# A decoder layer on one core: the end of the layer norms on GpSimd, two loads planned anew, and new due-time tables

## The chip, the cores and the metric

The kernel runs on one core of one Trainium2 chip. The metric is the device time of one execution in microseconds (us). A core has TensorE (PE in the profile, its weight loads PEld), VectorE (DVE), ScalarE (ACT), GpSimd (POOL) and SyncE (SP, which here issues nearly all DMAs). Each works through its own queue in order; they wait for each other by semaphores. TensorE writes PSUM, from which VectorE and ScalarE read.

## The reference

x has 4 sequences of 1024 rows of 256 elements. Three blocks follow each other, each on a layer norm without weights:

```python
x = x + attn(layernorm(x))              # causal, 16 heads of 16, cross + shifted scores mixed by a gate
x = x + xattn(layernorm(x), ctx, mask)  # 16 heads over 77 context rows
x = x + ffn(layernorm(x))               # silu(x wg) * (x wu), then wd; hidden size 768, integer weights
layernorm(x) = (x - mean(x)) / sqrt(var(x) + 1e-5)
```

## The kernel before

**Work and stages.** A chunk is 512 rows of one sequence, held as a tile of 128 partitions x 4 x 256; there are 8 chunks (b, n), b from 0 to 3, n 0 or 1. For each chunk the kernel runs:

- `project` (L780): norm of the rows, transposition, k, q and v projections. `spread_rows` (L756) makes each k or q tile: a projection on TensorE (L766), a high half on ScalarE (L729), a low half on VectorE (L732, L734), and eight DMAs on SP (L738) that spread the halves over the partitions.
- `maxima` (L838): scores for the row maxima (L866, causal mask L874), reduced by VectorE (L879); `shift` (L743) makes of them the tile that is subtracted in the next stage.
- `attend` (L903): scores again, keys on partitions (L949, shift L955, mask L962), exponentials on ScalarE (L968), weighted sums (L992, four heads in 32-column tiles), quotients (L679 to L685), output projection (L717) and the residual add on VectorE (L722). The residual x is loaded a second time (L919) and the output bias added on GpSimd (L922).
- `cross_attention` (L1052): norm, q projection and spread, masked maxima (L1106, L1114, L1120), exponentials (L1160, L1162), sums (L1173), output projection and add.
- `ffn` (L1187): norm, transposition into a high and a low half (L1207, L1209), gate and up (L1229), tanh on ScalarE (L1235), two products on VectorE (L1236, L1237), a high half on ScalarE (L1239), a low half on GpSimd (L1240), down (L1263), add (L1269), store (L1272). A first store of x (L1200) serves a branch that is not taken here.

**A norm** is `row_scales` (L148) and `normal_rows` (L163). VectorE takes statistics (L153, L154) of four slices and adds epsilon (L156); GpSimd raises to the power -0.5 (L158; in cross attention it also multiplies by a row mask, L160); VectorE then scales the four 128x256 slices (L166). `to_rows` (L177) transposes them on TensorE (L182).

**What sets the order.** The stages are Python generators. Each yields `piece`s: a TensorE duration, a list `use` of engine times behind it, a time `at` from which it may begin, and buffers that it takes (three PSUM pairs, two singles, six w4, three x and so on). `weave` (L467) keeps a model clock of every engine and always takes the piece that can begin first, moved by the stream's entry in the table LATES (L1290) for its chunk. So costs in `use`, `at` and the tables decide in which order TensorE's instructions are emitted, and that order is kept by hand. In the opening part, until the first maxima have begun, VectorE's order is kept too; after it the framework's scheduler orders the other engines by readiness. The norm's costs are in the list NORM (L696).

Of the kernel before, what the change touches and what calls it, by code (L numbers as in the profile page):

```python
# [8 lines left out]
F32 = mybir.dt.float32  # L9
# [5 lines left out]
ALU = mybir.AluOpType  # L15
# [4 lines left out]
P = 128  # L20
# [7 lines left out]
def tile_decoder_layer(  # L28
# [25 lines left out]
    nc = tc.nc  # L54

    B, S, D = x.shape
# [6 lines left out]
    NG = H // 4  # L63
    NHP = H // 2
    NT = S // P
    CH = 512
    NQ = S // CH
    QT = CH // P
# [16 lines left out]
    def pair():  # L85
        return pp.tile([P, 2, CH], F32, tag="pair", name="pair")

    def single():
        return ps.tile([P, CH], F32, tag="single", name="single")
# [28 lines left out]
    bo_b = const.tile([P, D], F32, name="bo_b")  # L118
# [15 lines left out]
    xpool = ctx.enter_context(tc.tile_pool(name="xpool", bufs=1))  # L134
    w4 = ctx.enter_context(tc.tile_pool(name="w4", bufs=6))
    small = ctx.enter_context(tc.tile_pool(name="small", bufs=2))
    xs = {}

    def x_rows(b, n):
        xt = wide([P, QT, D], "xr")  # L140
        nc.sync.dma_start(xt, x[b, n * CH : (n + 1) * CH, :].rearrange("(t p) d -> p t d", p=P))
        return xt

    def wide(shape, name, dt=F32):

        return w4.tile(shape, dt, tag="w4", name=name)
# [13 lines left out]
            nc.gpsimd.tensor_tensor(rs, rs, keep, ALU.mult)  # L160
        return mv, rs

    def normal_rows(xt, mv, rs, xn=None):  # L163
        xn = xt if xn is None else xn
        for i in range(QT):
            nc.vector.tensor_scalar(  # L166
                xn[:, i, :], xt[:, i, :], mv[:, i, 0:1], rs[:, i : i + 1],
                ALU.subtract, ALU.mult,
            )
        return xn  # L170

    def layer_norm(xt, keep=None):

        mv, rs = row_scales(xt, keep)
        return normal_rows(xt, mv, rs, wide([P, QT, D], "xn"))
# [11 lines left out]
    def transpose_rows(xn):  # L187
        t = to_rows(xn)
        xnT = wide([P, NC, CH], "xnT")
        nc.scalar.copy(xnT, t)  # L190
        return xnT
# [27 lines left out]
    x00 = x_rows(0, 0)  # L219
# [10 lines left out]
    x01 = x_rows(0, 1)  # L230
# [16 lines left out]
    for name, sgn in (("cm_qk", 1), ("cm_kq", -1)):  # L247
        t = masks_f[name] = stage.tile([P, P], BF16, name=name + "f")
# [55 lines left out]
    first = row_scales(x00)  # L304
    bvx = stage.tile([P, NC, P], F32, name="bvx")
    nc.vector.tensor_copy(bvx, bvn.unsqueeze(2).to_broadcast([P, NC, P]))
    normal_rows(x00, *first)

    def transposed(src, n, put):

# [16 lines left out]
    t = single()  # L327
# [3 lines left out]
    for ec in range(NC):  # L331
        t = single()
# [8 lines left out]
    t = single()  # L341
# [10 lines left out]
    t = single()  # L352
# [104 lines left out]
    def give(token, when):  # L457
        pool, k = token
        pool.free[k] = when

    def piece(pe, use=(), at=0.0, cond=None, free=(), mode="whole", **take):

        return dict(pe=pe, use=use, at=at, cond=cond, free=free, mode=mode, take=take)
# [227 lines left out]

        return rest

    NORM = [("DVE", 2.6), ("POOL", 1.1), ("DVE", 1.7)]  # L696

    def out_proj(st, nat, t_nat, w, xt):

# [80 lines left out]
    def project(st, b, n):  # L780

        if (b, n) == (0, 0):
            yield piece(0.0, w4=1)
            xnT, t_x, at = x00T, st.got["w4"], 0.0
        else:
            yield piece(
                0.0, use=[("DMA", 4.0)] * (b > 0) + NORM, w4=1,
                cond=lambda: (("half", b - 1) if b else ("projected", 0, 0, 0)) in flags,
            )
            t_xn = st.got["w4"]  # L790
            xn = x01 if (b, n) == (0, 1) else x_rows(b, n)
            normal_rows(xn, *row_scales(xn))
            flags.add(("normal", b, n))
            yield piece(
                1.1, use=[("ACT", 1.05)], at=st.done + LATE, pair=1, w4=1, free=t_xn
            )
            xnT = transpose_rows(xn)
            st.release("pair")
            t_x = st.got["w4"]
            at = st.done + LATE  # L800
        for c in range(NC):
            kT[b, n, c] = yield from spread_rows(
                st, wkT, xnT, c, bkp, (0, 1, 0, 1), 1.0, "k", at
            )
            qT[b, n, c] = yield from spread_rows(
                st, wqT, xnT, c, bqp, (0, 0, 1, 1), 1.0, "q", at, None,
                t_x if c == NC - 1 else (),
            )
            flags.add(("projected", b, n, c))
            if c == 0:  # L810
                for i in range(QT):
                    if i % 2 == 0:
                        yield piece(
                            2.0, use=[("ACT", 1.8)] if i else [],
                            cond=lambda: (b, n) != (0, 0) or ("normal", 0, 1) in flags,
                            **({} if i else {"pair": 1, "v": 1}),
                        )
                        if i == 0:
                            t_pair, t_v = st.got["pair"], st.got["v"][0]
                            vs = qk.tile(  # L820
                                [P, QT, H * V1 + W - V1], F32, tag="v", name="vs", bufs=NQ
                            )
                            nc.gpsimd.memset(vs, 1.0)
                            t = pair().rearrange("p a (i d) -> p (a i) d", d=D)
                    for k in range(NC):
                        nc.tensor.matmul(
                            t[:, i, :], xnT[:, k, i * P : (i + 1) * P], wvT[:, k, :],
                            start=(k == 0), stop=(k == NC - 1),
                        )
                give(t_pair.pop(), st.done)  # L830
                for i in range(QT):
                    nc.scalar.copy(
                        vs[:, i, : H * V1].rearrange("p (h w) -> p h w", w=V1)[:, :, 0:HD],
                        t[:, i, :].rearrange("p (h w) -> p h w", w=HD),
                    )
                vT[b, n] = vs, t_v, st.done + LATE
# [66 lines left out]
    def attend(st, b, n):  # L903
# [6 lines left out]
        for g in range(NG):  # L910
            c = g // 2
            if g % 2 == 0:
                yield piece(0.0, cond=lambda: (b, n, c) in shifts and (b, n) in vT and "selections" in flags)
                ms, at, t_ms = shifts.pop((b, n, c))
                if g == 0:
                    yield piece(0.0, x=1, use=[("DMA", 4.0)])
                    xt = xpool.tile([P, QT, D], F32, tag="x", name="x", bufs=3)
                    xs[b, n] = xt, st.got["x"][0]
                    nc.sync.dma_start(  # L919
                        xt, x[b, n * CH : (n + 1) * CH, :].rearrange("(t p) d -> p t d", p=P)  # L920
                    )
                    nc.gpsimd.tensor_tensor(  # L922
                        xt, xt, bo_b.unsqueeze(1).to_broadcast([P, QT, D]), ALU.add
                    )
                q, t_q, _ = qT.pop((b, n, c))
                over = [t_ms, t_q]
                if n == NQ - 1:
                    over += [kT[b, m, c][1] for m in range(NQ)]
            acc = []
            for kb in range(nk):  # L930
# [7 lines left out]
                for p in range(2):  # L938
                    yield piece(
                        0.04 + w * 8.2e-4 + (0.11 if diag else 0.0), mode="rows", pair=1, es=1,  # L940
                        at=at,
                        use=[("ACT", 0.1 + w * 1.85e-3)],
# [3 lines left out]
                    t = pair()  # L946
# [54 lines left out]
                lag.append(weigh)  # L1001
                if len(lag) > 1:
                    yield from lag.pop(0)()
                if tails and kb == 1:
                    nat, t_nat = yield from quotients(st, tails.pop(), nat, t_nat)
        yield from lag.pop()()
        nat, t_nat = yield from quotients(st, tails.pop(), nat, t_nat)
        yield from out_proj(st, nat, t_nat, woT, xt)
        flags.add(("attended", b, n))

    def quotients(st, tail, nat, t_nat):
        rest, toks, at, g = tail
        yield piece(
            0.55, use=[("DVE", 0.75)], at=at, single=1, free=toks,
            **({"w4": 1} if nat is None else {}),
        )
        if nat is None:
            nat, t_nat = wide([P, QT, D], "nat"), st.got["w4"][0]
        rest(nat, g)
        st.release("single")  # L1020
        return nat, t_nat
# [30 lines left out]
    def cross_attention(st, b, n):  # L1052
        yield piece(
            0.0, use=NORM, w4=1,
            cond=lambda: ("attended", b, n) in flags and "cross weights" in flags,
# [131 lines left out]
    def ffn(st, b, n, xt=None, rest=()):  # L1187
# [6 lines left out]
        yield piece(  # L1194
            0.0, use=NORM, w4=1, cond=lambda: ("crossed", b, n) in flags and all(("ffn weights", m) in flags for m in range(3)),
        )
# [82 lines left out]
    def every(part, lates, chunks=range(NQ)):  # L1279
# [8 lines left out]
        return Stream(pieces, lates)  # L1288

    LATES = (  # L1290
        [0.00, 0.00, 0.00, 0.00, -0.03, 0.00, -0.31, 0.00],
        [0.00, 0.00, 0.00, 0.00, 0.00, 0.00, -0.23, 0.00],
        [0.00, 0.00, 0.00, 0.00, 0.00, 0.00, 0.00, 0.00],
        [-1.02, 0.03, 0.00, -0.48],
        [0.54, 0.47, 0.00, 0.31],
        [-0.20, -0.15, -0.42, -0.02, 0.00, 0.33, 0.00, 0.00],
    )
    streams = [
        every(maxima, LATES[0]), every(cross_attention, LATES[1]), every(attend, LATES[2]),
# [13 lines left out]
    t = single()  # L1313
# [6 lines left out]
    with tc.If(over_v > 0):  # L1320
# [8 lines left out]
        for b in range(B):  # L1329
            for n in range(NQ):  # L1330
                xt = xpool.tile([P, QT, D], F32, tag="x", name="x", bufs=3)
# [35 lines left out]
```

## Time and profile before

| what | us |
|---|---|
| median of three timed runs | 1229.28 (1228.77 to 1231.69) |
| the profiled execution | 1232.86 |
| its span, first to last instruction | 1231.1 |
| TensorE busy | 1110.8 |
| VectorE busy | 729.9 |
| ScalarE busy | 562.6 |
| GpSimd busy | 130.8 |

The mean granted TensorE clock is 0.958. Busy time of TensorE is modelled from pipelined matmuls. In the profile a line of a group reads: line, engine, operation, tile written <- tiles read, shapes, count, busy time, mean ns of one, and the idle time of the engine ahead of them with what ended it. A line of the timeline reads: start, duration, engine, line, operation, tiles, shapes, count, and in brackets the idle time ahead of it and what ended that. In a line of the waits stand the waiting instruction, what it waited for, total us, times, longest.

### The profile page before, as it was taken

What the parts mean: (1) busy time and instruction counts of PE and PEld (TensorE: products, weight loads), DVE (VectorE), ACT (ScalarE), POOL (GpSimd) and SP (SyncE); (2) the same over time, 40 slices, a digit from 0 to 9 for tenths busy, and PEclk for the clock granted to TensorE, in tenths of its full rate; (3) what the DMA queues carried; (4) which work ended last, traced back from release to release, by engine and by line L of the source; (5) the groups of instructions that cost most, each with busy time, mean ns of one, the idle gap of its engine ahead of it and who ended that gap; (6) DMA issues with size and microseconds to landing.
All of it is one profiled execution on the core that took longest, in us unless ns stands there. A gap on an engine that the chain in (4) does not pass through costs nothing. (4 is left out here: it accounts for less than half of the span.)

```text
span 1231.1 us, 22029 instructions
## 1 busy us (share of the span) xinstructions
PE 1110.8 (90%) x9059; PEld 684.9 (56%) x9059; DVE 729.9 (59%) x1247; ACT 562.6 (46%) x801; POOL 130.8 (11%) x138
## 2 busy tenths in 40 slices
PE   6679989999999898999898998999999889996875
PEld 4445544557555466557555456556575545565654
DVE  5566786354687856255777856347458666136342
ACT  3044544654434463753353563653535336661521
POOL 4031000002000012001100002000110000011212
PEclk9798999999999999999999998999999989998986
DMA  6992315537732016555533015444826140006000
GB/s 124 130 201 63 58 33 69 69 53 92 97 55 40 9 38 110 75 71 87 87 52 38 8 42 70 85 63 60 102 44 91 36 63 8 18 1 86 1 35 19
DMA packets 65438, 76.44 MB, mean 62 GB/s; under 512 B 22451, under 2 KB 39399, under 8 KB 65332
## 3 DMA queue, kind: packets, MB, share of 16 engines
q1 hardware_dynamic: 64227, 74.62, 39.1%
q8 instruction: 73, 1.20, 0.5%
q10 hardware_dynamic: 1104, 0.35, 0.1%
q14 instruction: 34, 0.27, 0.1%
HBM read 15.28 MB, written 9.33 MB: 20 GB/s over the span
## 5 line engine op out<-in xcount | busy, mean ns | idle before, releaser
L968 ACT ACTIVATE es<-pair 128x1024 f32<-128x1024 f32 (+3 forms) x384 | 300.8, 812 | 252.6 <-PE pair L962 178.4
L879 DVE TENSOR_REDUCE mt<-pair 128x2 f32<-128x1024 f32 (+3 forms) x384 | 351.4, 952 | 92.3 <-PE pair L874 60.8
L866 PE MATMUL pair<-k,q 64*128 64x512 f32 (+3 forms) x768 | 163.2, 428 | 29.8 <-DVE mt L879 12.6
L949 PE MATMUL pair<-q,k 64*128 64x512 f32 (+3 forms) x768 | 161.4, 417 | 22.4 <-DVE mt L879 16.5
L992 PE MATMUL single<-es,vs 128*32 128x512 f32 (+3 forms) x1536 | 166.2, 506 | 0.1
L866 PEld LDWEIGHTS pair<-k,q 64*128 64x128 f32 x768 | 76.0, 188 | 121.4 <-DVE mt L879 41.7
L955 PE MATMUL pair<-ms,sel 64*128 64x512 f32 (+3 forms) x768 | 134.6, 347 | 0.0
L949 PEld LDWEIGHTS pair<-q,k 64*128 64x128 f32 x768 | 73.2, 187 | 102.6 <-issue 34.8
L1240 POOL TENSOR_TENSOR hT<-h,hT 128x512 fp32r<-128x512 f32 x48 | 61.4, 1280 | 306.8 <-ACT hT L1239 297.2
L1162 ACT ACTIVATE es<-pair 77x1024 f32<-77x1024 f32 x64 | 63.4, 1020 | 45.8 <-PE pair L1160 45.5
L955 PEld LDWEIGHTS pair<-ms,sel 64*128 64x128 f32 x768 | 74.2, 190 | 3.1
L1120 DVE TENSOR_REDUCE mx<-pair 128x8 f32<-128x616 f32 x64 | 48.7, 794 | 43.7 <-PE pair L1114 43.7
L1263 PE MATMUL pair<-wdT,hT 128*128 128x256 f32 x384 | 63.3, 320 | 11.6 <-POOL hT L1240 4.8
L158 POOL TENSOR_TENSOR rs<-ve,mhalf 128x4 f32<-128x4 f32 x24 | 24.3, 1012 | 439.5 <-DVE ve L156 439.4
L1235 ACT ACTIVATE h<-pair 128x512 f32<-128x512 f32 x48 | 28.7, 598 | 89.0 <-PE pair L1229 84.8
L874 PE MATMUL pair<-cm_qk,id 64*128 64x64 bf16 (+1 forms) x1024 | 69.0, 211 | 0.0
L962 PE MATMUL pair<-cm_kq,id 64*128 64x64 bf16 (+1 forms) x1024 | 67.3, 211 | 0.0
L1236 DVE SCALAR_TENSOR_TENSOR h<-h,pair 128x512 f32<-128x512 f32 x48 | 33.0, 687 | 57.5 <-ACT h L1235 57.2
L1263 PEld LDWEIGHTS pair<-wdT,hT 128*128 128x128 f32 x384 | 55.8, 216 | 18.4 <-POOL hT L1240 6.3
L1114 PE MATMUL pair<-k2s,q 128*128 128x156 f32 x256 | 46.7, 308 | 12.1 <-DMA q<-hi 5.3
L992 PEld LDWEIGHTS single<-es,vs 128*32 128x32 f32 x1536 | 32.4, 109 | 40.7 <-issue 29.6
L674 ACT COPY aS<-single 128x512 f32<-128x512 f32 x64 | 37.5, 589 | 31.6 <-PE single L992 19.0
(180 smaller groups left out, 1575.0 us busy)
## 6 DMA issues: line engine op xcount, KB each, us to landing
q<-hi SPq DMA_DIRECT2D x128, 128.0 KB, 5.1
q<-lo SPq DMA_DIRECT2D x128, 128.0 KB, 6.3
k<-hi SPq DMA_DIRECT2D x64, 128.0 KB, 4.3
k<-lo SPq DMA_DIRECT2D x64, 128.0 KB, 6.0
xr<-in_x_dram SPq DMA_DIRECT2D x8, 512.0 KB, 6.0
x<-in_x_dram SPq DMA_DIRECT2D x8, 512.0 KB, 7.4
x_dram<-x SPq DMA_DIRECT2D x8, 512.0 KB, 2.6
out_dram<-x SPq DMA_DIRECT2D x8, 512.0 KB, 3.7
```

What stands on the lines that cost most here:

```text
L866: nc.tensor.matmul(t[:, j, :w], q[r, a, i * P : (i + 1) * P], k[r, a, :w], start=True, stop=True,)
L874: nc.tensor.matmul(t[:, j, w - P + 64 * half : w], id2[r, half], cm_qk[r, half, 64 * half :], start=False, stop=True, skip_group_check=True,)
L879: nc.vector.tensor_reduce(mt[:, i, :, p, kc], t[:, :, :w], AX.X, ALU.max)
L949: nc.tensor.matmul(t[:, j, lo:], k[r, a, ki * P : (ki + 1) * P], q[r, a, lo:], start=True, stop=False,)
L955: nc.tensor.matmul(t[:, j, lo:], sel[r, hp, :], ms[r, lo:], start=False, stop=True)
L962: nc.tensor.matmul(t[:, j, lo : lo + 64 * (half + 1)], id2[r, half], cm_kq[r, half, : 64 * (half + 1)], start=False, stop=True, skip_group ...
L968: nc.scalar.activation(es[:, :, lo:], t[:, :, lo:], AF.Exp)
L992: nc.tensor.matmul(acc[0][W * jj : W * (jj + 1), lo:], vs[:, ki, V1 * h : V1 * h + W], both[jj // 2][:, jj % 2, lo:], start=(kb == 0), sto ...
L1120: nc.vector.tensor_reduce(mt[:, i, h4 : h4 + 4, :].rearrange("q (k p) j -> q k (p j)", k=2), tv[:, :, :, :S2], AX.X, ALU.max,)
L1162: nc.scalar.activation(es[:S2], t[:S2], AF.Exp)
L1240: nc.gpsimd.tensor_tensor(hs[:, 1, :], h, hs[:, 0, :].bitcast(F32), ALU.subtract)
L1263: nc.tensor.matmul(t[:, i, :], h[1][:, v, i * P : (i + 1) * P], w[:, h[0], :], start=(m == 0), stop=(m == len(terms) - 1),)
```

## The change

The scalings that end a norm move from VectorE to GpSimd, in the same queue as the root; only the very first chunk's norm keeps VectorE. The list NORM books this. In `project` the load of x is one piece, booked at 6.5 us where it was 4.0, and the norm's work a second piece that may begin when the load is done. In `attend` the piece that takes an x buffer and loads the residual stands after the first key block of the last head group and no longer at the stage's start, and the bias add is a piece of its own ahead of the last quotients. The entries of LATES are others.

```diff
-    def normal_rows(xt, mv, rs, xn=None):
+    def normal_rows(xt, mv, rs, xn=None, eng=nc.gpsimd):
         xn = xt if xn is None else xn
         for i in range(QT):
-            nc.vector.tensor_scalar(
+            eng.tensor_scalar(
                 xn[:, i, :], xt[:, i, :], mv[:, i, 0:1], rs[:, i : i + 1],
                 ALU.subtract, ALU.mult,
             )
...
-    normal_rows(x00, *first)
+    normal_rows(x00, *first, eng=nc.vector)
...
-    NORM = [("DVE", 2.6), ("POOL", 1.1), ("DVE", 1.7)]
+    NORM = [("DVE", 2.4), ("POOL", 3.4)]
...
             yield piece(
-                0.0, use=[("DMA", 4.0)] * (b > 0) + NORM, w4=1,
+                0.0, use=[("DMA", 6.5)] * (b > 0), w4=1,
                 cond=lambda: (("half", b - 1) if b else ("projected", 0, 0, 0)) in flags,
             )
             t_xn = st.got["w4"]
-            xn = x01 if (b, n) == (0, 1) else x_rows(b, n)
+            xn = x_rows(b, n) if b else x01
+            yield piece(0.0, use=NORM, at=st.done)
             normal_rows(xn, *row_scales(xn))
...
-                if g == 0:
-                    yield piece(0.0, x=1, use=[("DMA", 4.0)])
-                    xt = xpool.tile([P, QT, D], F32, tag="x", name="x", bufs=3)
-                    xs[b, n] = xt, st.got["x"][0]
-                    nc.sync.dma_start(
-                        xt, x[b, n * CH : (n + 1) * CH, :].rearrange("(t p) d -> p t d", p=P)
-                    )
-                    nc.gpsimd.tensor_tensor(
-                        xt, xt, bo_b.unsqueeze(1).to_broadcast([P, QT, D]), ALU.add
-                    )
...
                 if len(lag) > 1:
                     yield from lag.pop(0)()
+                if g == NG - 1 and kb == 0:
+                    yield piece(0.0, x=1, use=[("DMA", 6.5)])
+                    xt = xpool.tile([P, QT, D], F32, tag="x", name="x", bufs=3)
+                    xs[b, n] = xt, st.got["x"][0]
+                    nc.sync.dma_start(
+                        xt, x[b, n * CH : (n + 1) * CH, :].rearrange("(t p) d -> p t d", p=P)
+                    )
+                    x_at = st.done
...
         yield from lag.pop()()
+        yield piece(0.0, use=[("POOL", 1.5)], at=x_at)
+        nc.gpsimd.tensor_tensor(xt, xt, bo_b.unsqueeze(1).to_broadcast([P, QT, D]), ALU.add)
         nat, t_nat = yield from quotients(st, tails.pop(), nat, t_nat)
...
     LATES = (
-        [0.00, 0.00, 0.00, 0.00, -0.03, 0.00, -0.31, 0.00],
-        [0.00, 0.00, 0.00, 0.00, 0.00, 0.00, -0.23, 0.00],
-        [0.00, 0.00, 0.00, 0.00, 0.00, 0.00, 0.00, 0.00],
-        [-1.02, 0.03, 0.00, -0.48],
-        [0.54, 0.47, 0.00, 0.31],
-        [-0.20, -0.15, -0.42, -0.02, 0.00, 0.33, 0.00, 0.00],
+        [0.00, 0.00, 0.00, 0.00, -0.51, 0.00, 0.00, 0.00],
+        [0.00, -0.23, 0.00, 0.00, 0.00, 0.00, -0.05, -0.74],
+        [0.02, 0.00, 0.00, 0.00, 0.00, 0.00, 0.00, 0.04],
+        [0.43, -0.16, 0.00, -0.24],
+        [0.59, 0.33, 0.00, 0.14],
+        [0.00, 0.00, -0.63, -0.14, 0.00, 0.42, -0.76, 0.08],
     )
```

## The prediction

> **What bounds the kernel now.** I read the engine table first, then stretches, then who waited for whom, then the timeline at the largest holes.
>
> ```profile
> PE 1110.8 (90%) x9059; PEld 684.9 (56%) x9059; DVE 729.9 (59%) x1247; ACT 562.6 (46%) x801; POOL 130.8 (11%) x138
> ```
>
> ```profile
> 0.00:100.00 100.00, 72.08 (x531) 45.24 (x532) 59.51 (x125) 28.77 (x52) 25.51 (x46) 0.85 0.83 140
> 100.00:1100.00 1000.00, 943.22 (x8040) 567.53 (x8041) 609.47 (x1013) 498.10 (x696) 80.35 (x71) 0.98 0.38 58
> 1100.00:1231.00 131.00, 95.46 (x490) 72.13 (x489) 60.94 (x110) 35.73 (x53) 24.91 (x21) 0.85 0.18 33
> ```
>
> The second fence is busy time by stretch (columns PE, PEld, DVE, ACT, POOL, clock, DMA share, GB/s). TensorE sets the end: in the middle 1000 us it idles 56.8 us at a granted clock of 0.98; start and end hold another 28 and 36 us, at 0.85. VectorE is 59% busy, GpSimd 11%. So VectorE work taken away is worth only what TensorE waits for it.
>
> ```profile
> PE pair L949 <- DVE mt L879: 16.5, 22, 3.8
> PE pair L866 <- DVE mt L879: 12.6, 16, 3.2
> ...
> L166 DVE TENSOR_SCALAR xn<-x,mv,rs x64: 395/407/2407, 152.2 to 1187.4; 128x256 f32<-128x256 f32 x64
> ```
>
> Waits for the row maxima L879 are the largest group (us, times, longest): they free the PSUM pairs that TensorE writes next. The L166 row is the four scalings that end a norm: median 0.407 us, longest 2.407. The holes:
>
> ```profile
> 984.47 2.34 POOL L922 TENSOR_TENSOR x<-x,bo_b 128x1024 f32<-128x1024 f32 x1
> 984.55 3.38 DVE L166 TENSOR_SCALAR xn<-x,mv,rs 128x256 f32<-128x256 f32 x4 [0.95 <-POOL rs L160]
> 988.59 0.79 PE L949 MATMUL pair<-q,k 64*128 64x512 f32 x2 [3.80 <-DVE mt L879]
> ...
> 480.25 0.64 PE L1114 MATMUL pair<-k2s,q 128*128 128x156 f32 x4 [2.60 <-DMA q<-lo]
> 763.01 1.11 PE L1114 MATMUL pair<-k2s,q 128*128 128x156 f32 x4 [2.94 <-issue]
> ...
> 1187.03 1.94 PE L182 MATMUL pair<-ident,xn 128*128 128x128 f32 x8 [4.93 <-DVE xn L166]
> ```
>
> At 984 VectorE waits 0.95 us for GpSimd's root, then one scaling lasts as long as the GpSimd add beside it (2.41 against 0.41 us), the maxima queue behind, and TensorE stands for 3.80 us. A like hole of 1.85 us ends at 198.31. The two L1114 holes are something else: the q that cross attention spreads by DMA has not landed. At 1187 the last norm lies bare on the path.
>
> **Off VectorE (gain).** 23 of 24 norms lose 4 x 0.407 = 1.63 us of VectorE each, 37 us in all, its waits for the root (22 us) and the twelve stretched scalings (12 us over their median, each beside a GpSimd instruction). Nearly all of that has cover: around most norms TensorE does not idle at all. I count the two holes that end in it, **-5.7 us**; bounds 0 (the maxima are late again) and -23 us (every middle hole that ends at L879).
>
> **Onto GpSimd (cost).** No row shows such a scaling on GpSimd. One-input rows of L641 (1.04, 0.83, 0.62 us for 1024, 768, 512 elements) give 0.41 us for 256; the two-input rows L922 and L1240 (2.37 and 1.28 us) give 0.74. I take 0.55, nearer the one-input rows since only one operand is a tile: 2.2 us for four, between 1.6 and 2.9. A norm's path from the last L717 matmul becomes add 1.22 + statistics 2.4 + root 1.0 to 1.2 + 2.2 = 7.0 us, 0.6 longer than with VectorE. The new TensorE order, laid out with the trace's spacings (0.23 us a feed-forward matmul, 0.43 an L717 one), puts 11 us or more between that matmul and the transposes, 8.6 at the last cross attention: covered. Bare is only the last norm: **+0.4** (transposes follow the scalings one by one; -0.2 to +1.0).
>
> The Trainium skill (GPSIMD Engine Reference, "Engine selection") speaks against the move: elementwise work belongs on VectorE, GpSimd being about twice as slow with two inputs and near line rate with one. By twice the VectorE row the four would last 3.3 us, an estimate that adds 1.1 us at the last norm alone: the sum would be a microsecond smaller.
>
> What queues behind: GpSimd also makes the low halves L1240 (48 x 1.28 us), for which TensorE waits 4.8 us now. With 50 us more on a 131 us queue, these waits grow: **+2** (0 to +12, if each of 24 pairs met half a microsecond).
>
> **Another order on TensorE.** The tables and the new pieces re-plan everything; the two orders hold the same matmuls line by line (1792 of maxima, 2560 of scores, 1152 + 1152 of feed-forward). Two things can be counted.
>
> First, changes of array layout (64-row tiles, 32-column tiles, whole array) fall from 681 to 634. The trace prices them as start-to-start time beyond the median spacing: leaving columns 0.35 us, rows to columns 0.08, rows to whole 0.12, whole to rows 0.03. With 4, 8, 14 and 25 fewer (and 4 more from whole to columns at 0.03): 1.4 + 0.6 + 1.7 + 0.8 - 0.1 = **-4.4 us**; bounds 0 (waits lie in these means) and -6.
>
> Second, the distance from a q projection to its first use. In the two L1114 holes the projection ended at 468.3 and 751.0 and the data landed 12.0 us later, with only 8.5 us of TensorE work ordered between. In the new order the shortest such distance in the middle is 11.6: **-5.5 us** (-6 to 0, if other q tiles come late in turn). At the last cross attention the two distances go from 6.7 and 5.9 to 7.6 and 7.8 us against holes of 5.33 and 1.26 us: **-1.0** (-2 to 0).
>
> Against it, the PSUM pairs are taken more densely: stretches in which four are claimed within about 2 us of TensorE work rise from 251 to 286 (middle). Now TensorE waits 34 us in the middle for L879, L968 and L1162 to free a pair, 0.135 us per such stretch: 35 x 0.135 = **+4.7** (0 to +9).
>
> **The start.** The second chunk's v projection (3.40 and 1.99 us before 62 us, at a low clock) and its last k projection (1.98 at 62.8) move behind the first exponentials: 6.0 us at full clock. Walking VectorE's rows forward (eight maxima, 3.5 us of selections, q's low half, seven maxima, a 1.2 us maximum of weights, k's) the first exponential comes at 63 instead of 65.3. Left are 4 us, half of which fit the 6.9 us that TensorE idles from 65 to 100: **+2** (-2 to +6).
>
> **x read late, costs of transfers.** Nothing by themselves: the load of x is still issued when one of three buffers comes free, in the same neighbourhood of SP's queue (behind the output store of an earlier chunk), and the add stays on GpSimd. Its 155.9 us of waiting there (longest 43.8) held no norm up: VectorE never waited more than 1.5 us for a root. The booked 6.5 us fit the measured landings (6.0 and 7.4).
>
> **Sum**: -5.7 + 0.4 + 2 - 4.4 - 5.5 - 1.0 + 4.7 + 2 = -7.5 us. The profiled execution took 1232.86 (span 1231.1 and 1.8 around it), 3.6 above the median 1229.28; it would become 1225.4, the median 1221.8.
>
> **Rivals.**
> *The holes go and nothing fills them*: without the 4.7 and the two costs of 2 the sum is -16.2, with 2 more from L879 -18: 1229.3 - 18 = 1211. For it: VectorE gets 60 us freer just where maxima queue. Against: TensorE is at 94% there.
> *The waits only move*: the denser pair use and new late q tiles take back what the old holes gave, 1229. For it: such a plan is made from booked durations, and 144 small holes now sit all over the middle.
> *GpSimd's queue becomes the wait* (slower): it works in order, and in the new order five of the eight adds of x stand directly ahead of a norm. A norm has about 4 us of slack (11 less 7.0); an add whose transfer is still under way takes up to 7.4 + 2.37, so 5.8 us of TensorE each. Three such: 1221.8 + 17.4 = 1239; from two on it decides. Against: the same five neighbourhoods exist now without harm.
>
> **Chances.** Forecast 0.46 (own range 1216 to 1226), nothing fills the holes 0.16, waits only move 0.16, GpSimd's queue 0.22. About 0.3%, 3.7 us, is what a measurement of this kernel can tell from no change. Faster 0.44 + 0.16 = 0.60; same 0.16 + 0.02 = 0.18; slower 0.22. The range 1209 to 1240 leaves out the outer ends of the first and last rival, under 2 in 10.
>
> **What will show it.** L166 on GpSimd at 0.41 to 0.74 us; no stretched scaling on VectorE; VectorE near 681 us busy, GpSimd near 181; middle idle of TensorE from 57 to some 52 us (the layout changes pass as busy time), with no 2.6 us hole ahead of L1114; first exponential before 65 us; the last bare norm hole 4.7 to 5.9 us. Wrong, if transposes L182 wait for GpSimd, if L1263 waits for L1240 by more than 10 us, or if the middle idles over 60 us.

## The result and the profile after

The changed kernel takes 1261.67 us (median of four, 1260.21 to 1268.34) where the kernel before takes 1229.03 beside it: 1.0271 times as long (95% interval 1.0232 to 1.0310), 32.6 us slower. The forecast was 1221.8, range 1209 to 1240. Its profiled execution took 1261.28 us, with a span of 1259.5 against 1231.1.

Line numbers of the changed kernel are one higher than before's from L788 on, nine lower in the scores of `attend` (scores L940, exponentials L959, weighted sums L983), and one higher again behind them (bias add L1007, products L1237 and L1238, low half of h L1241, down L1264).

The engine table's first line, and the busy time by stretch (columns PE, PEld, DVE, ACT, POOL, clock, DMA share, GB/s):

```profile
PE 1110.7 (88%) x9059; PEld 682.5 (54%) x9059; DVE 690.0 (55%) x1155; ACT 561.7 (45%) x801; POOL 241.9 (19%) x230
```

```profile
0.00:100.00 100.00, 68.93 (x544) 42.62 (x545) 58.29 (x126) 28.86 (x51) 30.26 (x50) 0.88 0.73 130
100.00:1100.00 1000.00, 922.79 (x7829) 553.75 (x7828) 570.81 (x922) 483.68 (x679) 171.04 (x146) 0.98 0.39 59
1100.00:1260.00 160.00, 119.00 (x689) 86.12 (x689) 60.92 (x108) 49.12 (x72) 40.65 (x34) 0.88 0.16 31
```

TensorE does the same work in the same busy time at the same clock: 1110.7 us for 9059 matmuls. VectorE got 40 us freer, as meant. But in the middle 1000 us TensorE now idles 77.2 us where it idled 56.8. Between its first and its last matmul its holes grew from 105.0 to 132.3 us, and these 27.3 are nearly all of the 28.4 us that the span grew. The time went into waits. Who waited for whom in the changed kernel, then two rows of the kernel before:

```profile
PE pair L867 <- DVE mt L880: 17.0, 29, 2.7
PE pair L940 <- DVE mt L880: 15.8, 26, 2.9
PE pair L182 <- POOL xn L166: 15.0, 15, 5.7
...
PE pair L867 <- DVE h L1238: 6.0, 4, 2.1
```

```profile
PE pair L182 <- DVE xn L166: 6.1, 2, 4.9
...
PE pair L1263 <- POOL hT L1240: 4.8, 6, 1.0
```

The waits for row maxima, which the freer VectorE was to shorten, stand at 32.8 us in these two rows instead of 29.1. Transposes wait 15.0 us for GpSimd's scalings where they waited 6.1 for VectorE's. A wait that was small before, for the product h on VectorE, holds the maxima's scores up. Summed over all waiting lines, holes ended by h went from 2.2 to 10.6 us, by cross attention's maxima mx from 1.9 to 6.7, by the packed maxima mpad from 0.6 to 5.9. In the middle 1000 us alone, holes ended by the maxima grew from 23.1 to 31.0 us.

The row of the scalings (least, median, longest ns):

```profile
L166 POOL TENSOR_SCALAR xn<-x,mv,rs x64: 1217/1220/1227, 151.3 to 1216.2; 128x256 f32<-128x256 f32 x64
```

One takes 1.220 us, 3.0 times VectorE's 0.407 and more than twice the 0.55 that I took. Four and the root last about 6 us; the changed NORM books 3.4.

The start, and the last norm, in TensorE's timeline:

```profile
60.61 0.89 PE L747 MATMUL single<-ident,mpad 128*128 128x128 f32 x4 [4.74 <-DVE mpad L888]
...
1213.89 0.69 PE L182 MATMUL pair<-ident,xn 128*128 128x128 f32 x2 [5.75 <-POOL xn L166]
1215.10 0.69 PE L182 MATMUL pair<-ident,xn 128*128 128x128 f32 x2 [0.52 <-POOL xn L166]
```

The first is a new hole. The last norm's hole grew from 4.93 to 5.75 us, and after the first transposes TensorE stands about half a microsecond for each further scaling.

### The profile page after: what moved, and what is told of

Its sections match the earlier page's. It is cut to its first block, busy times and chain, and to the rows that moved or that the text cites. A ratio compares the mean times of both kernels' runs of the same rounds, so it can differ in the third digit from the quotient of the medians.

```text
span 1259.5 us, 22081 instructions
## 1 busy us (share of the span) xinstructions
PE 1110.7 (88%) x9059; PEld 682.5 (54%) x9059; DVE 690.0 (55%) x1155; ACT 561.7 (45%) x801; POOL 241.9 (19%) x230
## 4 chain that ended last, share of the span: by engine, by line
PE 33%; DVE 9%; POOL 4%; issue 3%; ACT 3%; DMA 2%; SPq 0%; POOLq 0%; ACTq 0%; DVEq 0%
PE single L983 5%; DVE mt L880 5%; PE pair L940 4%; PE single L766 3%; PE pair L867 2%; PE pair L1161 2%; PE pair L717 2%; POOL xn L166 2%; PE pair L946 2%; PE pair L1230 2%; PE pair L1264 2%; DMA q<-lo 2%; PE single L679 2%; PE pair L182 1%; PE single L1174 1%
## 5 line engine op out<-in xcount | busy, mean ns | idle before, releaser
L959 ACT ACTIVATE es<-pair 128x1024 f32<-128x1024 f32 (+3 forms) x384 | 300.5, 811 | 253.7 <-PE pair L953 179.9
L940 PE MATMUL pair<-q,k 64*128 64x512 f32 (+3 forms) x768 | 160.8, 416 | 22.9 <-DVE mt L880 15.8
L983 PE MATMUL single<-es,vs 128*32 128x512 f32 (+3 forms) x1536 | 163.5, 497 | 0.5 <-ACT aS L674 0.5
L940 PEld LDWEIGHTS pair<-q,k 64*128 64x128 f32 x768 | 72.4, 185 | 105.8 <-issue 44.3
L1241 POOL TENSOR_TENSOR hT<-h,hT 128x512 fp32r<-128x512 f32 x48 | 61.2, 1275 | 267.8 <-ACT hT L1240 243.0
L166 POOL TENSOR_SCALAR xn<-x,mv,rs 128x256 f32<-128x256 f32 x64 | 77.3, 1221 | 1.7
L1264 PE MATMUL pair<-wdT,hT 128*128 128x256 f32 x384 | 62.2, 316 | 9.1 <-POOL hT L1241 3.8
L1237 DVE SCALAR_TENSOR_TENSOR h<-h,pair 128x512 f32<-128x512 f32 x48 | 32.9, 686 | 66.0 <-ACT h L1236 65.9
L953 PE MATMUL pair<-cm_kq,id 64*128 64x64 bf16 (+1 forms) x1024 | 66.7, 209 | 0.0
L684 DVE RECIPROCAL rd<-single 128x16 f32<-128x16 f32 x64 | 16.2, 254 | 88.5 <-PE single L679 88.4
L1264 PEld LDWEIGHTS pair<-wdT,hT 128*128 128x128 f32 x384 | 54.9, 213 | 15.1 <-POOL hT L1241 5.1
L1007 POOL TENSOR_TENSOR x<-x,bo_b 128x1024 f32<-128x1024 f32 x8 | 18.9, 2366 | 212.7 <-DMA x<-in_x_dram 179.1
```

Of the source, the lines that this page charges most:

```text
L166: eng.tensor_scalar(xn[:, i, :], xt[:, i, :], mv[:, i, 0:1], rs[:, i : i + 1], ALU.subtract, ALU.mult,)
L940: nc.tensor.matmul(t[:, j, lo:], k[r, a, ki * P : (ki + 1) * P], q[r, a, lo:], start=True, stop=False,)
L953: nc.tensor.matmul(t[:, j, lo : lo + 64 * (half + 1)], id2[r, half], cm_kq[r, half, : 64 * (half + 1)], start=False, stop=True, skip_group ...
L959: nc.scalar.activation(es[:, :, lo:], t[:, :, lo:], AF.Exp)
L983: nc.tensor.matmul(acc[0][W * jj : W * (jj + 1), lo:], vs[:, ki, V1 * h : V1 * h + W], both[jj // 2][:, jj % 2, lo:], start=(kb == 0), sto ...
L1241: nc.gpsimd.tensor_tensor(hs[:, 1, :], h, hs[:, 0, :].bitcast(F32), ALU.subtract)
```

## The experiments

Two things changed at once: which engine scales, and the order in which everything is emitted, since `piece`s, bookings and tables all feed the planner. My first theory was **price**: the loss is GpSimd's 1.220 us, booked too low. The rival was **order**: the re-planned order is slower whoever scales. Times are medians; ratios are to the kernel before on the same chip, with 95% intervals.

### Price or order

**e1_after_vector** keeps the changed kernel's order of TensorE, ScalarE and SyncE, with the scalings on VectorE.

```diff
-    def normal_rows(xt, mv, rs, xn=None, eng=nc.gpsimd):
+    def normal_rows(xt, mv, rs, xn=None, eng=nc.vector):
```

> The changed kernel with its scalings L166 back on VectorE; booked costs, tables and so the order of TensorE, ScalarE and SyncE are those of the changed kernel, instruction by instruction. Theory (price): the four scalings on GpSimd, 4.9 us where the plan books 2.4, make the loss of 32 us; with VectorE (1.63 us) most of it goes: 1225 to 1238. Rival (order): the new order of TensorE is itself worse, whoever scales: 1250 to 1262. In between, both have a part.

Measured: 1261.17 us, 1.0251 (1.0205 to 1.0297). **Price** falls: the same order without any scaling on GpSimd is as slow. Its waits show what the order does alone:

```profile
PE pair L867 <- DVE mt L880: 18.6, 30, 2.7
PE pair L940 <- DVE mt L880: 17.6, 27, 4.1
...
PE pair L867 <- DVE h L1238: 8.0, 4, 3.5
PE pair L1115 <- DMA q<-lo: 6.2, 2, 4.4
```

The wait for xn is back at its old size (6.1 us), but those for maxima (36.2 in two rows against 29.1) are longer than in either kernel. Those for q, both halves over all lines, are 17.0 us against 16.5 in either. So in this order GpSimd's scalings do shorten the waits for maxima, from 39.0 to 35.4 us over all lines, and lengthen those of the transposes, from 7.9 to 18.6; the medians do not differ.

**e2_before_gpsimd** is the reverse: before's order, with the scalings (all but the first chunk's) on GpSimd.

```diff
-    def normal_rows(xt, mv, rs, xn=None):
+    def normal_rows(xt, mv, rs, xn=None, eng=nc.gpsimd):
...
-            nc.vector.tensor_scalar(
+            eng.tensor_scalar(
```

> The kernel before with nothing changed but the engine of the scalings (GpSimd but for the first chunk); the order of TensorE, ScalarE and SyncE is that of the kernel before. Theory (price): each norm gets 3.2 us longer in an order made for the short norm, so about as much is lost as in the changed kernel: 1248 to 1265. Rival (order): GpSimd's price is hidden there, 1229 to 1236.

Measured: 1244.71 us, 1.0117 (1.0069 to 1.0164). That lies between the ranges of the two theories: in before's order GpSimd's price is 15.6 us, half the loss. e2's waits:

```profile
PE pair L182 <- POOL xn L166: 17.9, 17, 5.7
PE pair L1263 <- POOL hT L1240: 13.0, 7, 4.4
PE pair L866 <- DVE mt L879: 12.7, 17, 3.2
PE pair L949 <- DVE mt L879: 11.1, 20, 0.7
```

My gain is there to the tenth: holes ended by the maxima over all lines fell from 31.5 to 25.8 us, 5.7, and the two holes that I had counted are the ones that went. It is outweighed at xn (17.9 against 6.1) and at the low half hT (13.0 against 4.8). GpSimd's timeline of e2 shows how the second comes about:

```profile
469.11 3.63 POOL L166 TENSOR_SCALAR xr<-xr,mv,rs 128x256 f32<-128x256 f32 x3
472.70 1.26 POOL L1240 TENSOR_TENSOR hT<-h,hT 128x512 fp32r<-128x512 f32 x1
473.95 1.22 POOL L166 TENSOR_SCALAR xr<-xr,mv,rs 128x256 f32<-128x256 f32 x1
```

Three scalings hold the queue for 3.63 us, the low half comes after them, and TensorE's down projection stands for 4.37 us where it stood 0.63.

**e4_forms** asks what the 1.220 us consists of. Each of a norm's four scalings has another form, so the rows are not normalised: two operations with per-partition operands (as the change has it), one such operation, two operations with constants, one with a constant.

```diff
+            elif i == 1:
+                eng.tensor_scalar(xn[:, i, :], xt[:, i, :], rs[:, i : i + 1], None, ALU.mult)
+            elif i == 2:
+                eng.tensor_scalar(xn[:, i, :], xt[:, i, :], 0.01, 1.01, ALU.subtract, ALU.mult)
+            else:
+                eng.tensor_scalar(xn[:, i, :], xt[:, i, :], 1.01, None, ALU.mult)
```

> The changed kernel with four forms of scaling in one norm, to price them on GpSimd: slice 0 as it is (two operations, two scalars read from SBUF), slice 1 one multiplication by a scalar read from SBUF, slice 2 two operations with constants, slice 3 one multiplication by a constant. Slices 1 to 3 leave out the true mean and scale, so the output is another. If the 1.22 us lies in the scalars read from SBUF, slice 0 is 1.22, slice 1 about 0.8 and slices 2 and 3 about 0.41, as the one-input rows of the casts say; if each operation costs a pass, slices 0 and 2 are 1.22 and slices 1 and 3 about 0.6 to 0.7; if it is the price of a scaling in any form, all are 1.22.

The four forms on GpSimd (count | busy us, mean ns | idle before):

```profile
L167 POOL TENSOR_SCALAR xn<-x,mv,rs 128x256 f32<-128x256 f32 x16 | 19.7, 1230 | 1.7
...
L174 POOL TENSOR_SCALAR xn<-x 128x256 f32<-128x256 f32 x16 | 17.3, 1083 | 180.0 <-DVE x L729 180.0
L172 POOL TENSOR_SCALAR xn<-x,rs 128x256 f32<-128x256 f32 x16 | 14.9, 930 | 0.0
L176 POOL TENSOR_SCALAR xn<-x 128x256 f32<-128x256 f32 x16 | 13.7, 858 | 0.0
```

None of the three cases that I had set out came. The plainest form, one operation with a constant, already takes 858 ns. A second operation adds 0.23 to 0.30 us, per-partition operands 0.07 to 0.15. The casts from which I took 0.41 us are no neighbours of this instruction.

**e3_booked_6** tells the changed kernel's planner the truth and leaves its tables.

```diff
-    NORM = [("DVE", 2.4), ("POOL", 3.4)]
+    NORM = [("DVE", 2.4), ("POOL", 6.1)]
```

> The changed kernel with 6.1 us booked for GpSimd's part of a norm (root 1.0, mask 0.2, four scalings 4.9) instead of 3.4; tables kept. Theory (price): once the plan knows the price it puts other work ahead of the transposes and gets part of the loss back: 1238 to 1255, and TensorE waits less than 5 us for L166 outside the last norm (15 and 3.5 us in the changed kernel). Rival (order): no better than 1255 to 1270.

Measured: 1336.86 us, 1.0875 (1.0830 to 1.0920). A true booking made it 75 us slower still. No theory had that: the planner answers to a small change of cost with another order altogether.

### One part at a time

That gave a third theory, **fit**: six rows of tables are right for one set of costs and pieces only, and any other pair of them draws an order with more holes. Rivals: **tables** (the new rows are bad) and **late x** (reading x late costs).

**f1_tables_only**: before with the new LATES, nothing else. **f2_after_old_tables**: the changed kernel with the old LATES, scalings on VectorE. Both swap the block of the change's diff. **f3_late_x_only** and **f4_pieces_only** take over, with the old LATES and VectorE, the hunk of `attend`, or the hunks of NORM and `project`.

> The kernel before with the changed kernel's six rows of LATES and nothing else (x early, one norm piece with its old bookings, scalings on VectorE). 'Fit' theory (tables and bookings are good only together, any new pair of them draws another order that idles more): 1240 to 1265 us. 'Tables' rival (the new rows themselves are bad): 1255 to 1270 here, and the run with the old rows in the changed kernel falls back to about 1229. 'Late x' rival (the late read carries the loss): within 5 us of 1229.

> The changed kernel with the old rows of LATES and with its scalings on VectorE (so to be set beside the 1261 us of the changed order with VectorE). 'Fit': still slower than before, 1240 to 1290 us, since the rows no longer fit the pieces. 'Tables': 1229, within 5. 'Late x': 1255 to 1265, as with the new rows.

> The kernel before with x for the sums read late (load issued after the last scores of a chunk, the add of bo in a piece of its own behind the last weighted sums), old rows, old norm piece, VectorE. 'Late x': 1250 to 1262 us, with the wait for L1007's add or for GpSimd on its path. 'Tables': within 5 us of 1229. 'Fit': 1235 to 1260, with the idle time spread over the waits for row maxima and for q's low half and none of it at x.

> The kernel before with the norm's piece split in two (transfer booked 6.5 us, then root and scalings at its landing, booked DVE 2.4 and POOL 3.4), old rows, x early, scalings still on VectorE. 'Fit': 1235 to 1265 us. 'Tables' and 'late x': within 5 us of 1229.

| | us | ratio |
|---|---|---|
| f1, new tables alone | 1292.62 | 1.0517 (1.0474 to 1.0561) |
| f2, all but the tables | 1352.70 | 1.1011 (1.0981 to 1.1041) |
| f3, late x alone | 1331.94 | 1.0838 (1.0809 to 1.0867) |
| f4, norm pieces and bookings alone | 1313.78 | 1.0705 (1.0675 to 1.0734) |

Every part alone loses 65 us or more, and the parts together without the tables 125. So the new tables are no culprit: they bring the new pieces from 1352.7 to 1261. Only fit had all four slow, and all four lie above its ranges too. Part of the size goes with the clock, as f2's stretches show against before's 0.85 and 0.98:

```profile
0.00:100.00 100.00, 63.26 (x420) 40.28 (x420) 51.29 (x116) 23.48 (x43) 23.81 (x45) 0.81 0.83 136
100.00:1200.00 1100.00, 981.19 (x8050) 591.13 (x8048) 611.77 (x1020) 495.87 (x696) 81.72 (x73) 0.95 0.35 53
```

f2's TensorE is busy 1156.7 us for the same 9059 matmuls that took 1110.8, and idle for 195.3 us of its span where before's is for 120.3. Its mean granted clock is 0.923 for 0.958. The five versions that idle most, e3 and f1 to f4 (157.6 to 195.3 us), were granted 0.923 to 0.943 in their profiled executions, all others 0.944 to 0.961. That the idle time brings the clock down is not shown.

### Other tables for the same code

Is the changed code slower by itself, or only as far as its tables go? I ran the kernel's own `weave` with many tables and kept those whose planner clock (the end of its last piece, a number of the planner and not a time of the chip) was near that of the two kernels, 1220.9 for before and 1217.0 for the change. For e3 it stands at 1297.9 and for f1 to f4 at 1322.3, 1320.9, 1323.1 and 1308.8: the planner itself finds these orders long, so they say little of the changed kernel, whose order it finds short and which is slow on the chip all the same. Only rows of LATES differ within a code and its bookings:

```diff
-        [-1.02, 0.03, 0.00, -0.48],
-        [0.54, 0.47, 0.00, 0.31],
+        [0.00, 0.00, 0.02, -0.25],
+        [0.03, 0.04, 0.13, 0.38],
```

(two of the six rows, for g3). g1 and h2 also book the change truly, NORM on GpSimd 6.1 and the add of bo 2.4; g2 puts the scalings on VectorE; g4 has x early.

> Control: the kernel before, nothing changed but LATES, found anew from zeros by the planner's clock until it stood at 1220.0 us there (before's own rows: 1220.9). 'Fit': 1240 to 1265 us, although code and bookings are before's. 'Misbooked' and 'change's own cost': 1222 to 1237.

> A second set of rows found by the planner's clock for the code of before, at 1224.6 us there; the first, at 1220.0, took 1239.9. 'Fit': 1235 to 1270. 'Change's own cost': 1225 to 1245, below both sets of the changed code.

> The changed kernel with its bookings set to what the trace shows (NORM on GpSimd 6.1 instead of 3.4, the x add 2.4 instead of 1.5) and LATES found anew for these bookings by the planner's own clock (1225.5 us there; 1217.0 for the changed kernel, 1220.9 for before). 'Misbooked' theory (the changed plan loses because it holds GpSimd's norms for shorter than they are): the waits of L182 for GpSimd fall from 18.5 to under 10 us and the time returns to 1225 to 1240. 'Fit' theory (a plan that is found on the planner's clock alone comes out 20 to 45 us above that clock on the chip, whatever its norms do): 1240 to 1270. 'Change's own cost' rival (late x, or GpSimd behind the root, costs 30 us in any order): 1255 to 1270, with this run slower than the control with before's code by 20 or more.

> A second set of rows of LATES for the changed kernel with true bookings (6.1 and 2.4), at 1218.8 us on the planner's clock; the first, at 1225.5, took 1248.2. 'Fit': anything from 1235 to 1270, unlike the first by 5 us or more, so that the set of rows and not the norms decides. 'Change's own cost': 1248 to 1262, and both sets above both sets of before's code.

> The changed kernel with its own bookings (NORM on GpSimd 3.4) and other rows of LATES, at 1213.2 us on the planner's clock, 3.8 below the changed kernel's rows. If the planner's clock could rank plans this near each other, 1257; 'Fit': anywhere from 1240 to 1280. 'Misbooked': as slow as the changed kernel or slower, with 15 us or more of waiting for L166 again.

> Late x and the split norm piece as in the changed kernel, but the scalings on VectorE, booked as three steps (DVE 2.4, POOL 1.1, DVE 1.7), and LATES found anew for that (1215.0 us on the planner's clock). 'Misbooked': near 1229, within 8. 'Fit': 1235 to 1265, no matter that nothing is misbooked. 'Change's own cost', if it lies in late x: 1250 to 1270; if it lies in GpSimd's scalings: 1229 or below.

> x early and one norm piece as before, scalings on GpSimd booked 6.1 as measured, LATES found anew for that (1217.4 us on the planner's clock). Beside before's order with GpSimd's scalings unbooked (1244.7): 'misbooked': 1225 to 1238, the L182 waits for GpSimd under 10 us. 'Fit': 1240 to 1265. 'Change's own cost' in GpSimd's scalings: 1245 to 1260; in late x: 1225 to 1240.

| code | tables | planner's clock | us | ratio |
|---|---|---|---|---|
| before | its own | 1220.9 | 1229.03 | 1 |
| before | g3 | 1220.0 | 1239.88 | 1.0057 (1.0031 to 1.0082) |
| before | h3 | 1224.6 | 1270.45 | 1.0325 (1.0282 to 1.0369) |
| changed | its own | 1217.0 | 1261.67 | 1.0271 (1.0232 to 1.0310) |
| changed | h4 | 1213.2 | 1264.97 | 1.0281 (1.0238 to 1.0324) |
| changed, true bookings | g1 | 1225.5 | 1248.19 | 1.0136 (1.0104 to 1.0168) |
| changed, true bookings | h2 | 1218.8 | 1268.79 | 1.0318 (1.0269 to 1.0368) |
| late x, VectorE | g2 | 1215.0 | 1257.50 | 1.0223 (1.0189 to 1.0258) |
| early x, GpSimd | g4 | 1217.4 | 1260.62 | 1.0231 (1.0207 to 1.0255) |

Before's code with another table (h3) is as slow as the change, and no faster than either truly booked set, against "change's own cost". Three sets of rows within 5 us of each other on the planner's clock lie 41 us apart on the chip for before's code, and two sets 7 us apart lie 21 apart for the truly booked change; the planner's lowest takes 1265, its highest 1248. That agrees with fit, though g3 lies just below its range. True bookings did not reliably help, and g1's transposes still wait 15.7 us for GpSimd where "misbooked" had under 10, so "misbooked" is not shown. h3's waits have a familiar row:

```profile
PE pair L949 <- DVE h L1237: 11.3, 2, 6.0
```

It is the wait for h that the changed kernel has grown too, in code that changed nothing but tables.

To see where a planner's promise breaks, I set each piece's planned start beside the start of its matmuls in the trace (lag in us):

| trace time near | before | changed | e1 | g3 | h3 |
|---|---|---|---|---|---|
| 300 | 15.9 | 26.7 | 28.2 | 18.0 | 35.9 |
| 600 | 16.4 | 38.7 | 43.7 | 28.6 | 44.8 |
| 960 | 20.8 | 53.6 | 57.8 | 37.6 | 59.2 |

Before's order falls 5 us further behind through the middle; the four others fall behind by 20 to 30. No single place loses the time: the holes are many, and they lie in waits that the planner's model thinks met. Which part of the model is wrong was not tested.

### The change in before's order

**k1_late_x_kept_order** issues x's load and add late without moving a piece, so that TensorE's order is before's exactly; **k2_both_kept_order** adds GpSimd's scalings.

```diff
                 if g == 0:
                     yield piece(0.0, x=1, use=[("DMA", 4.0)])
-                    xt = xpool.tile([P, QT, D], F32, tag="x", name="x", bufs=3)
...
+                if g == NG - 1 and kb == 0:
+                    xt = xpool.tile([P, QT, D], F32, tag="x", name="x", bufs=3)
...
         yield from lag.pop()()
+        nc.gpsimd.tensor_tensor(xt, xt, bo_b.unsqueeze(1).to_broadcast([P, QT, D]), ALU.add)
```

> Late x without a re-plan: TensorE's order is before's to the instruction, the piece that takes x's buffer stays where it was, and only the load is issued after the chunk's last scores and its add of bo behind the last weighted sums; scalings on VectorE. 'Fit': 1225 to 1234, late x as such costs nothing (the same edit with its own pieces took 1332). 'Change's own cost' in late x: 1240 or more, with TensorE or VectorE's L722 add waiting for GpSimd's add of bo.

> The same with the scalings on GpSimd: all that the change does to the code, in before's order. 'Fit' with GpSimd's price beside it: 1238 to 1250, near the 1244.7 of GpSimd's scalings alone in that order; a few us less if the x adds no longer stand ahead of the norm at 993 us, where GpSimd's scalings cost 3.1 us. 'Change's own cost' by the two together: 1255 or more.

Measured: k1 1241.43, 1.0103 (1.0052 to 1.0154); k2 1251.18, 1.0160 (1.0102 to 1.0217). Here fit missed: late x costs some 13 us by itself. The profiled executions lie only 6.4 us apart, so the size is known to some microseconds only. It is one hole, in the start. VectorE's, then TensorE's timeline of k1, then a row of SyncE's queue in before and the one that stands at the same time in k1:

```profile
71.55 1.22 DVE L643 TENSOR_REDUCE big<-wi 128x1 f32<-128x1024 f32 x1 [12.90 <-POOL wi L641]
72.69 1.22 DVE L879 TENSOR_REDUCE mt<-pair 128x2 f32<-128x1024 f32 x1
73.94 0.18 DVE L887 COPY mpad<-mt 128x32 f32<-128x32 f32 x1
```

```profile
74.18 1.11 PE L747 MATMUL single<-ident,mpad 128*128 128x128 f32 x4 [10.96 <-DVE mpad L887]
```

```profile
61.53 1.75 SPq L919 DMA_DIRECT2D x<-in_x_dram  x1
```

```profile
61.53 1.69 SPq L639 DMA_DIRECT2D wi<-in_L_ffn_w_gate_dram  x1
```

Before issues two loads of x there, at 57.7 and 61.5 us. With the second gone, the load of the feed-forward weights takes its place (81.4 us in before), their cast follows on GpSimd, and VectorE's reduction of them (L643) stands ahead of the last maximum before mpad. The load is issued at 61.5 us, the cast ends at 71.5, VectorE stands 12.90 us for it, and the packed maxima that TensorE needs lie behind. Before has the same reduction at 89 us, clear of mpad. In the changed kernel it is the 4.74 us hole at 60.6: there VectorE waits 2.80 us for the same cast at 57.3. From the first exponential to the last weighted sum k1 idles 59.9 us against before's 63.6: behind the start late x cost no idle time. k2 lies just above the range that fit had for it (1238 to 1250 us), and under the 1255 of the change's own cost.

### The stretched scalings

**h1_before_two_holes** tests the gain I had forecast, inside before's order: one norm's scalings on GpSimd (the one behind the hole of 1.85 us), and the add of bo in four.

```diff
-                    nc.gpsimd.tensor_tensor(
-                        xt, xt, bo_b.unsqueeze(1).to_broadcast([P, QT, D]), ALU.add
-                    )
+                    for i in range(QT):
+                        nc.gpsimd.tensor_tensor(xt[:, i, :], xt[:, i, :], bo_b, ALU.add)
...
+            normal_rows(xn, *row_scales(xn), eng=nc.gpsimd if (b, n) == (1, 1) else nc.vector)
```

> Before's order of TensorE, ScalarE and SyncE, with two edits: the GpSimd add of bo to x as four instructions of 256 columns instead of one of 1024, and the scalings of one norm (the one at 195 us) on GpSimd. If a VectorE scaling lasts as long as the GpSimd instruction beside it, the one at 984 us falls from 2.41 to at most 0.7 us and its hole from 3.80 to about 2.1; the hole of 1.85 us at 196.5 us goes. Together 3.6 us, 1225 to 1227 us where before stands at 1229. If the stretch comes of something else, the 984 us scaling stays above 2 us and the time within 1 us of before.

Measured: 1228.68 us, 0.9984 (0.9959 to 1.0009): no difference that can be told. The 1.85 us hole went. The other shrank only from 3.80 to 3.39, as VectorE's and GpSimd's timelines show:

```profile
985.05 2.98 DVE L166 TENSOR_SCALAR xn<-x,mv,rs 128x256 f32<-128x256 f32 x4 [0.94 <-POOL rs L160]
```

```profile
984.96 2.91 POOL L923 TENSOR_TENSOR x<-x,bo_b 128x256 f32<-128x256 f32 x4
```

Four short adds went hand in hand with four scalings, 0.73 us each; the sum is nearly the old one. The Trainium skill (SBUF — State Buffer, "SBUF: two separate sides") has a rule that fits: of a GpSimd instruction and a VectorE one that needs the port pair they share (in a two-port mode, or with two inputs from SBUF), the one that starts first holds the pair for its whole length, and the other waits. The trace agrees: of 13 scalings beside a GpSimd instruction in before, 12 are stretched, to between 1.12 and 2.41 us, one to 2.407 beside an add of 2.344; the thirteenth, at 0.40 us, had begun 0.26 us ahead of GpSimd's. No run was made with the add on another engine.

TensorE's holes fell by 3.6 us in h1's profiled execution and the median by 0.8: gains of this size are at the limit of what can be measured here. h1 is the only version that comes out level with before; none beats it.

## Why the prediction was wrong

- **Another order on TensorE** is the step that failed. It said "two things can be counted" and came, with pair use and the start, to -4.2 us. The same order with VectorE's scalings (e1) measured about +32, x read late included. Layout changes (-4.4) showed no gain in TensorE's busy time (1110.7 us for 1110.8; 1117.2 in e1, at a lower clock). The L1114 holes in the middle did go, but q's waits as a whole, the hole at 763.01 among them, fell only from 19.4 to 16.5 us: that of the start is 7.5 us for 5.6, and new ones of 1.67 and 0.67 stand near 623 us. Pair use (+4.7, 0 to +9) was mis-sized: in the middle 1000 us the waits ended by L879, L968 and L1162 were 33.9 us in before and 48.0 in e1, +14.1; in the changed kernel they were 43.7, with the gain of "Off VectorE" already in them. Put at nothing without a reason were the waits for h, mx and mpad, +18.5 us together over the span. I counted what I could see in the old holes, when the old order, as it turned out, was the fastest of all that were run. (The prediction's 1152 + 1152 matmuls of feed-forward hold those of the branch that is not taken; the trace has 384 + 384 in either kernel.)
- **Onto GpSimd** took 0.55 us (0.41 to 0.74) for a scaling that takes 1.220. Casts and adds did not bound it. The rule of the Trainium skill (GPSIMD Engine Reference, "Engine selection") that spoke against the move was nearer than my rows: twice VectorE's time is 0.81 us, an estimate by that page, and the runs show 3.0 times. GpSimd came to 241.9 us busy for 181. The bare last norm came to +0.8 us and three gaps of half a microsecond behind it, for +0.4.
- **Off VectorE**, -5.7, was right as idle time (e2: 31.5 to 25.8). As time it was not shown: h1 took 3.6 us of holes away and moved the median 0.8, its interval reaching from -5.0 to +1.1 us.
- **What queues behind**, +2 at L1240: +8.2 in before's order (e2), -1.0 in the new one.
- **x read late**, "nothing by themselves": wrong at the start. My walk of VectorE's rows held the 1.2 us of L643 ahead of mpad, but not that the load of the feed-forward weights comes forward when one of x leaves, nor the wait for their cast (2.80 us). The first exponential begins at 66.7 us; by the same row before's begins at 66.8, not 65.3, so it did not come earlier.
- **VectorE** came to 690.0 for 681, since other instructions grew (mask tiles xpad and mneg by 2.0, in e1 as well) and overlapping rows had been subtracted twice: the scalings that left held 44.6 us of VectorE, not 49. No stretched scaling is left, as forecast.
- The **rival** on the slower side had the sign, with another mechanism: no root waits behind an x add in the new order; two wait 4.2 us behind another norm's four scalings, and transposes wait for the scalings themselves. Two of the three signs named for being wrong came: transposes wait for GpSimd (18.6 us), the middle idles over 60 (77.2). L1263's wait for L1240 stayed at 3.8.

Not settled is how much of the changed kernel's 32.6 us each part owns. In before's order, GpSimd's scalings alone cost 15.6, late x alone 13 and both 23; in the changed order GpSimd's cost nothing net; the parts do not add. Why an order that the planner finds short runs long on the chip stays open, wait by wait. Nor is it shown that no tables exist that make the changed code as fast as before: three sets besides its own took 1248 to 1269. How before's own rows were found is not on record; if by trial on the chip, that alone would make them hard to match.

## What to carry to other kernels

Where a planner draws the order, a change of pieces, costs or tables is first of all a new draw: price it by what other draws of the same code take on the chip, not by the holes of the old one that it happens to remove. Test the idea inside the old order before planning anew. Before moving work to another engine, time that very form on it; a cast or an add of the same size is no stand-in.

## What the runs showed of the hardware

- GpSimd's tensor_scalar on 128x256 fp32 takes 0.858 us with one operation and a constant (e4) and 1.220 with two operations and per-partition operands; VectorE's takes 0.407 in the latter form.
- A VectorE scaling that starts beside a running GpSimd instruction lasts until that instruction, or the one right behind it, is done (12 in before, 1.12 to 2.41 us where the median is 0.407); four scalings beside four adds of 0.73 us were all caught (2.98 us, h1).
- TensorE's busy time for the same matmuls rose from 1110.8 to 1156.7 us in the order with the most idle time (f2), at a granted clock of 0.81 in the first 100 us and 0.95 behind them.
